# A two-layer decoder block on one core: the first layer's mixer, cross attention and routing issued in turns on half blocks, the shared expert divided over two places

## The chip, the cores and the metric

The kernel runs on one core of one Trainium2 chip. The metric is device time in microseconds (us) for one execution, the median of several runs. A profile is one execution recorded by the hardware profiler; its engines are PE (matmuls, with weight loads counted apart as PEld), DVE (vector), ACT (scalar and activation), POOL (general purpose) and SP (issues most transfers). "PE clock" is the share of full clock that the chip granted to PE.

## The reference

Input x is 64 sequences of 64 tokens with 256 features, all float32, and a context of 64 x 64 x 64. Two layers follow one another, each with three residual steps on a layer norm of x:

```python
x = x + ssm(layernorm(x))            # layer 0 mixer: in_proj, conv over 4 tokens, silu, chunked scan, out_proj
x = x + cross_attn(layernorm(x), ctx)# layer 0: 16 heads against the rotated context
x = x + moe(layernorm(x))            # layer 0: top 2 of 7 experts, and one shared expert for all tokens
x = x + rwkv(layernorm(x))           # layer 1: time mixing, a max-stabilised scan
x = x + gqa(layernorm(x), ctx, ctx)  # layer 1: 32 query heads, 8 key/value heads
x = x + ffn(layernorm(x))            # layer 1: 64 experts in 8 groups, dense over the groups
```

Each expert of `moe` is `down(silu(gate(u)) * u)` with `u = up(h)`, with a bias in each of the three. An expert's result is scaled by its token's probability; the shared expert's result is not.

## The kernel before

x (4096 tokens) stays in on-chip memory as 32 tiles of 128 tokens. A block is 512 tokens (`TB`, 8 blocks, `NBLK`), a half block 256 (`HT` in the new code). Matmul results go to PSUM tiles that rotate through one tag (`mm`); cross attention also had a tag of double size (`big`).

Three phases make the first layer, one after the other (`run`, `phase`, `moe_phase`). In them the program states work in a pipeline's order, and the framework's scheduler decides in what order instructions stand on each engine.

- **Mixer** (to 395 us). `ssm_front` works on a block: layer norm and RMS norm (`norm`, on POOL, L107), transposes (`transposed`, L116), projections of 512 columns (`proj`, L210), convolution (`acc`, ACT L236, DVE L239), softplus (L169 to L180), Silu (L240, L242). Then per tile `ssm_mix`, `ssm_scan` and `ssm_out`. The weights of cross attention are combined beside it (`prep_xattn`).
- **Cross attention** (395 to 810 us). `xattn_front` per block: the rotated context `kv` and its transpose, the norm (`ln_T`), queries (`q_ps`, L374). Per tile `xattn_scores`, `xattn_turn`, `xattn_values`, `xattn_out` (L414). Meanwhile `moe_clear` writes zeros over the whole row buffer `moe_hs` in DRAM, 30 pieces of 1088 KB.
- **Experts** (810 to 1229 us). `moe_front` routes a block: norm, transposes, router logits (`pl`, L496), choice of two experts on DVE (L503 to L509), ranks within each expert by two matmuls (`rk`, L519, L520), probabilities, slots. Eight scatters on POOL (L541) then put each row into its expert's part of `moe_hs`. When all blocks are routed, `moe_tables` computes which expert each tile of 256 slots belongs to. `moe_fetch` reads two numbers of that table on SP, then loads the rows (`ht`) and the expert's weights (`pack`). There are 38 routed tiles (`MAXT`) with stages `moe_turn`, `moe_up` (L618), `moe_gate` (L627), `moe_down` (L638, L646), which write `moe_ys` in DRAM. The shared expert is 16 further tiles in the same stages: 14 ahead of the routed ones, beside the routing, and 2 after. All biases of the last product come by one more matmul with the probabilities (`prT`, `moe_bd`, L640).

The second layer (`layer1`) follows from 1229 us on. It is issued by hand: inside `manual_schedule()` every engine executes in program order. Each part is a generator that yields between pieces, and `beside` takes pieces from several generators in proportion to the counts given. First `collect_block(0)` gathers expert results into x (L693, POOL), then `wkv(0)` runs alone, then `wkv(1)` beside `gqa(0)`; these make the ramp, to 1441 us. After that `ffn_block(b)`, `wkv(b + 2)` and `gqa(b + 1)` run beside one another. `ffn_front` at the end of `gqa` makes the norm `fr_h` on POOL (L1022), its transposes (L1028), and the gating, with waiting turns (`rest`) between its pieces.

Of the kernel before, what the change touches and what calls it, by code (L numbers as in the profile page):

```python
# [6 lines left out]
F32 = mybir.dt.float32  # L7
# [6 lines left out]
P = 128  # L14
# [5 lines left out]
HB = NB // 2  # L20
NBLK = 8
LN_EPS = 1e-5
# [4 lines left out]
SLOTS = NBLK * TB  # L27
ET_PER_E = SLOTS // ET
MAXT = (2 * SLOTS + 7 * (ET - 1)) // ET
# [13 lines left out]
class Net:  # L43
# [32 lines left out]
    def big(self, shape, name):  # L76

        return self.pp.tile(shape, F32, tag="big", bufs=self.n_big, name=name)

    def open_psum(self, n_big):  # L80
        self.n_big, self.n_mm = n_big, 8 - 2 * n_big
        self.pp = self.tc.alloc_tile_pool(name="psum", bufs=1, space=PSUM, reuse_waits="tile")
# [21 lines left out]
    def norm(self, wk, blk, rs, nm, eng):  # L104
        h = wk.tile([P, NT, D], F32, tag="h", bufs=2, name="h")
        for t in range(NT):
            eng.tensor_scalar(h[:, t], self.x[:, blk * NT + t], rs[:, t:t + 1], nm[:, t:t + 1], ALU.mult, ALU.add)  # L107
        return h

    def transposed(self, h):  # L110

        out = []
        for c in range(2):
            ps = self.mm([P, TB], "hT_ps")
            for t in range(NT):
                self.nc.tensor.transpose(ps[:, t * P:(t + 1) * P], h[:, t, c * P:(c + 1) * P], self.ident)  # L116
            out.append(ps)
        return out

    def ln_T(self, wk, blk, eng):  # L120
        nc = self.nc
        mv, rs = self.stats(wk, blk * NT)
        nm = self.neg_mean_times(wk, mv, rs)
        h = self.norm(wk, blk, rs, nm, eng)
        ps = self.transposed(h)
        hT = wk.tile([P, 2, TB], F32, tag="hT", bufs=2, name="hT")
        nc.scalar.copy(hT[:, 0], ps[0])  # L127
        nc.vector.tensor_copy(hT[:, 1], ps[1])
        return hT
# [30 lines left out]
    def softplus(self, wk, dt, raw):  # L160

        nc = self.nc
        sh = [P, NT, 4]

        def t(n):
            return wk.tile(sh, F32, tag="sp_" + n, bufs=2, name="sp_" + n)
# [15 lines left out]
    def ssm_front(self, wk, w, blk):  # L182
        nc, te = self.nc, self.nc.tensor
        mv, rs = self.stats(wk, blk * NT)
        nm = self.neg_mean_times(wk, mv, rs)

        r2 = wk.tile([P, NT], F32, tag="r2", bufs=2, name="r2")
        nc.vector.tensor_mul(r2, rs, rs)
        nc.vector.tensor_mul(r2, r2, mv[:, :, 1])
        nc.vector.tensor_scalar(r2, r2, RMS_EPS, None, ALU.add)  # L190
        rr = wk.tile([P, NT], F32, tag="rr", bufs=2, name="rr")
        nc.gpsimd.tensor_tensor(rr, r2, self.mhalf, ALU.pow)
        nc.vector.tensor_mul(rr, rr, rs)
        nr = self.neg_mean_times(wk, mv, rr, "ln_nr")
        h = self.norm(wk, blk, rr, nr, nc.gpsimd)
        r1 = wk.tile([P, NT], F32, tag="r1", bufs=2, name="r1")
        nc.vector.tensor_scalar(r1, rs, 1.0, None, ALU.add)
        ps = self.transposed(h)
        hT = wk.tile([P, 2, TB], F32, tag="hT", bufs=2, name="hT")
        nc.scalar.copy(hT[:, 0], ps[0])  # L200
        nc.vector.tensor_copy(hT[:, 1], ps[1])

        for t in range(NT):
            n = blk * NT + t
            nc.gpsimd.tensor_scalar(self.x[:, n], self.x[:, n], r1[:, t:t + 1], nm[:, t:t + 1], ALU.mult, ALU.add)

        def proj(col):
            ps = self.mm([P, TB], "proj")
            for c in range(2):
                te.matmul(ps, w["in"][:, c, col:col + P], hT[:, c], start=c == 0, stop=c == 1)  # L210
            return ps


        pdt = self.mm([P, NT, 4], "pdt")
        for t in range(NT):
            for c in range(2):
                te.matmul(pdt[:, t], hT[:, c, t * P:(t + 1) * P], w["in"][:, c, 1024:1028], start=c == 0, stop=c == 1)
        raw = wk.tile([P, NT, 4], F32, tag="raw", bufs=2, name="raw")
        nc.vector.tensor_add(raw, pdt, bc(w["dtb"], 1, NT))
        dt = wk.tile([P, NT, 4], F32, tag="dt", bufs=2, name="dt")  # L220
        self.softplus(wk, dt, raw)
        la = wk.tile([P, NT, 4], F32, tag="la", bufs=2, name="la")
        nc.vector.tensor_mul(la, dt, bc(w["A"], 1, NT))

        bT = wk.tile([P, TB], F32, tag="bT", bufs=2, name="bT")
        cT = wk.tile([P, TB], F32, tag="cT", bufs=2, name="cT")
        nc.scalar.copy(bT, proj(1028))
        nc.vector.tensor_copy(cT, proj(1156))

        sg = wk.tile([P, 4, TB], F32, tag="sg", bufs=2, name="sg")  # L230
        xs = wk.tile([P, 4, TB], F32, tag="xs", bufs=2, name="xs")
        g2 = wk.tile([P, 4, TB], F32, tag="g2", bufs=2, name="g2")
        for q in range(4):
            px = proj(512 + q * P).rearrange("p (b s) -> p b s", s=S)
# [104 lines left out]
    def xattn_kv(self, wk, w, blk):  # L339
# [5 lines left out]
        for j in range(2):  # L345
            self.load(c2[j * S:(j + 1) * S], cv)
# [1027 lines left out]
```

## Time and profile before

| what | us |
|---|---|
| median of 3 runs (2395.75 to 2404.59) | 2399.03 |
| the profiled execution, its whole time | 2401.51 |
| its span, first to last instruction | 2399.7 |
| PE busy over the span | 2084.6 (87%) |
| DVE, ACT, POOL busy | 1257.5, 775.1, 804.0 |
| mean PE clock granted | 0.929 |

An engine's busy time is the union of its instructions' intervals. A group's mean is the duration of one instruction; matmuls overlap in the pipeline, so a 256-column matmul lasts 379 ns while the next starts 215 ns after it. A float32 matmul stands as two records. "Idle before" is how long the engine had nothing before an instruction, with what released it.

### The profile page before, as it was taken

The numbers are of one execution on the slowest core, as the hardware profiler recorded it, in microseconds if no ns is written. First come the engines' busy times: TensorE is split into PE (matmuls) and PEld (weight loads), VectorE is DVE, ScalarE is ACT, GpSimd is POOL, SyncE is SP. The second block draws the span as 40 slices with busy tenths as digits, with TensorE's granted clock in tenths as the row PEclk, the third lists the DMA queues.
The fourth block names the chain that finished last, engine by engine and source line by source line (L and its number), as shares of the span: only waits on it lengthen the run. The fifth ranks groups of instructions, "written<-read, shape, count | busy, mean of one in ns | idle before, by whom it ended". The sixth has DMA issues, their size and how long they took to land.

```text
span 2399.7 us, 32463 instructions
## 1 busy us (share of the span) xinstructions
PE 2084.6 (87%) x12586; PEld 1487.4 (62%) x12586; DVE 1257.5 (52%) x2832; ACT 775.1 (32%) x1398; POOL 804.0 (34%) x1047
## 2 busy tenths in 40 slices
PE   6899998999999667999954659888898989898989
PEld 3566665566666556888853446556666656565666
DVE  5565566544444433333326556555666656665332
ACT  2232241222223243333312214334342434353421
POOL 4434435322222353011144634252525243332100
PEclk8899999999999768999986779999999999999999
DMA  4111006660000111367751101010101010000000
GB/s 136 32 31 31 1 1 200 190 214 5 1 1 1 37 70 50 119 223 242 232 147 28 25 3 19 8 25 5 30 6 29 3 23 12 12 6 12 6 5 11
DMA packets 111514, 133.81 MB, mean 56 GB/s; under 512 B 31866, under 2 KB 100610, under 8 KB 111362
## 3 DMA queue, kind: packets, MB, share of 16 engines
q1 hardware_dynamic: 96034, 104.48, 14.2%
q0 software_dynamic: 15328, 27.27, 4.5%
q8 instruction: 99, 1.62, 0.3%
q14 instruction: 53, 0.43, 0.1%
HBM read 75.23 MB, written 56.49 MB: 55 GB/s over the span
## 4 chain that ended last, share of the span: by engine, by line
PE 53%; DVE 16%; POOL 13%; issue 13%; ACT 3%; DMA 1%; POOLq 0%; DVEq 0%; SPq 0%; ACTq 0%
PE gu_ps L1096 10%; PE proj L210 5%; PE q_ps L374 4%; PE acc L1130 4%; POOL x_sb L693 3%; PE po L414 3%; PE po L280 2%; PE sc L384 2%; POOL moe_hs L541 2%; PE pc L408 2%; PE st L935 2%; PE gu_ps L1102 2%; DVE ln_st L91 1%; PE wk_po L839 1%; POOL ln_rs L96 1%
## 5 line engine op out<-in xcount | busy, mean ns | idle before, releaser
L1096 PE MATMUL gu_ps<-ffn_gu,hT 128*128 128x352 f32 x1024 | 333.7, 472 | 7.3 <-DVE gqa_q L924 6.9
L1096 PEld LDWEIGHTS gu_ps<-ffn_gu,hT 128*128 128x128 f32 x1024 | 192.1, 195 | 109.3 <-issue 12.0
L1107 DVE SCALAR_TENSOR_TENSOR a<-a,fr_sca,gu_ps 128x176 f32<-128x176 f32 x256 | 84.6, 392 | 165.1 <-ACT a L1106 164.8
L1130 PE MATMUL acc<-ffn_d,aT 128*128 128x256 f32 x704 | 166.0, 385 | 0.0
L210 PE MATMUL proj<-hT,w_in 128*128 128x512 f32 x320 | 146.8, 616 | 0.0
L1130 PEld LDWEIGHTS acc<-ffn_d,aT 128*128 128x128 f32 x704 | 130.6, 192 | 20.2 <-issue 4.5
L1106 ACT ACTIVATE a<-gu_ps 128x176 f32<-128x176 f32 x256 | 60.5, 322 | 235.7 <-PE gu_ps L1102 235.7
L629 DVE TENSOR_TENSOR gT<-gT,uT 128x512 f32<-128x512 f32 x54 | 37.4, 692 | 166.7 <-ACT gT L628 166.7
L393 POOL TENSOR_TENSOR p<-p,sm 128x1024 f32<-128x1024 f32 x32 | 60.9, 1902 | 186.1 <-DVE sm L392 186.1
L414 PE MATMUL po<-xa_vo,ctxT 128*128 128x256 f32 x512 | 117.6, 379 | 0.0
L374 PE MATMUL q_ps<-hT,xa_q 128*128 128x512 f32 x256 | 113.8, 602 | 1.5 <-ACT hT L127 1.4
L414 PEld LDWEIGHTS po<-xa_vo,ctxT 128*128 128x128 f32 x512 | 96.3, 190 | 25.8 <-issue 12.2
L693 POOL DMA_INDIRECT x_sb<-moe_ys,left x64 | 102.6, 1604 | 21.3 <-issue 18.7
L647 POOL DMA_DIRECT2D moe_ys<-y x38 | 27.2, 717 | 238.3 <-DVE y L646 231.3
L210 PEld LDWEIGHTS proj<-hT,w_in 128*128 128x128 f32 x320 | 61.8, 197 | 72.3 <-issue 69.2
L924 DVE TENSOR_REDUCE gqa_q<-sc 128x8 f32<-128x512 f32 x128 | 79.3, 681 | 23.3 <-PE sc L922 22.8
L961 POOL TENSOR_TENSOR x_sb<-x_sb,at 128x256 f32<-128x256 f32 x32 | 24.8, 776 | 197.7 <-DVE at L960 197.7
L541 POOL DMA_INDIRECT moe_hs<-moe_h,moe_slots x64 | 62.3, 974 | 74.8 <-issue 35.5
L255 POOL TENSOR_TENSOR ul<-ssm_U,la 128x512 f32<-128x512 f32 x32 | 34.0, 1064 | 158.0 <-PE pld L257 158.0
L374 PEld LDWEIGHTS q_ps<-hT,xa_q 128*128 128x128 f32 x256 | 48.4, 192 | 61.6 <-issue 55.6
L96 POOL TENSOR_TENSOR ln_rs<-ln_ve,mhalf 128x4 f32<-128x4 f32 x40 | 40.9, 1022 | 118.8 <-DVE ln_ve L94 100.9
L938 ACT ACTIVATE pT<-st 128x512 f32<-128x512 f32 x128 | 66.1, 602 | 38.0 <-PE st L935 37.8
(334 smaller groups left out, 4677.5 us busy)
## 6 DMA issues: line engine op xcount, KB each, us to landing
moe_hs<-moe_zero SPq DMA_DIRECT2D x30, 1088.0 KB, 11.2
pack<-in_moe_pack_dram SPq DMA_DIRECT2D x38, 770.0 KB, 5.5
ht<-moe_hs SPq DMA_DIRECT2D x38, 272.0 KB, 2.9
moe_ys<-y POOLq DMA_DIRECT2D x38, 256.0 KB, 5.6
c<-in_ctx_dram SPq DMA_DIRECT2D x40, 128.0 KB, 3.5
x_sb<-in_x_dram SPq DMA_DIRECT2D x8, 512.0 KB, 8.7
out_dram<-x_sb SPq DMA_DIRECT2D x32, 128.0 KB, 1.7
ffn_gu<-in_ffn_guT_dram SPq DMA_DIRECT2D x8, 352.0 KB, 7.9
```

What stands on the lines that cost most here:

```text
L96: nc.gpsimd.tensor_tensor(rs, ve, self.mhalf[:, 0:nt], ALU.pow)
L210: te.matmul(ps, w["in"][:, c, col:col + P], hT[:, c], start=c == 0, stop=c == 1)
L374: te.matmul(ps, wq[:, c, hp * P:(hp + 1) * P], hT[:, c], start=c == 0, stop=c == 1)
L393: nc.gpsimd.tensor_mul(p, p, bc(sm, 2, S))
L414: self.nc.tensor.matmul(po, st["cT"][:, hp], w["vo"][:, hp], start=hp == 0, stop=hp == 7)
L541: s = gp.indirect_dma_start(w["hs"], bass.IndirectOffsetOnAxis(w["slots"][:, b, k, i:i + 1], 0), ha[k][:, i], None).ins
L693: self.nc.gpsimd.indirect_dma_start(self.x[:, b * NT + i], None, self.ys, bass.IndirectOffsetOnAxis(self.left[:, b, k, i:i + 1], 0), compu ...
L924: v.tensor_reduce(st["qa"][:, :, k, 16:18], sc[k], AX.X, ALU.max, negate=True)
L938: self.nc.scalar.activation(pT[:, k], ps[k].rearrange("p j g s -> p j (g s)"), AF.Exp, scale=8.0 ** -0.5)
L1096: te.matmul(ps, f["hT"][:, c, tok], w["gu"][:, 4 * q + j, c], start=c == 0, stop=False)
L1107: v.scalar_tensor_tensor(a[:, e], a[:, e], f["sca"][:, k:k + 1], pg[j][:, 176:352], ALU.mult, ALU.mult)
L1130: self.nc.tensor.matmul(self.acc, aT, w["d"][:, k], start=k == 0, stop=k == 10)
```

## The change

The three phases of the first layer become one function `layer0` inside `manual_schedule()`, so every engine follows program order there. It takes 18 steps (`NH + XLAG`, `NH` = 16 half blocks). In step n it issues, in proportion: the mixer of half block n with the front of half n + 1, cross attention of half n - 2 with the front of half n - 1, and half of the routing of a block whose halves are done. In the first two steps the combination of cross attention weights runs in place of cross attention. All tiles are sized to a half block: projections and queries are 256 columns wide, two to a PSUM tile; cross attention's PSUM tiles of double size are divided. Norms of mixer and cross attention move to ACT (`normed`); `kv` is kept in two standing tiles that are cleared once.

The routing of blocks 0 to 6 thus lies in `layer0`; block 7's comes at the start of `moe_phase`. Each routed block's transposed rows are stored to DRAM (`hTd`) and loaded again by the shared expert. `moe_clear` goes: two pieces are cleared at the start, and `moe_tables` scatters 14 rows-of-zero tiles behind the last row of each expert. The bias matmuls and `prT` go: a routed tile loads its expert's bias (with the shared one added), DVE adds it and ACT scales. The shared expert has 6 tiles (`EARLY`) ahead of the routed ones, and 10 in `moe_rest`, issued beside the ramp of the second layer. The last layer's weights are loaded inside that ramp (`load_ffn`). In `moe_phase` SP alone follows program order. In `ffn_front` one waiting turn between `fr_h` and its transposes becomes four.

```diff
+EARLY = 6
+NH = 2 * NBLK
+XLAG = 2
-    def ssm_front(self, wk, w, blk):
+    def ssm_front(self, wk, w, n0, f):
...
+        def proj(*cols):
+            ps = self.mm([P, 2, HT], "proj")
+            for i, col in enumerate(cols):
+                for c in range(2):
+                    te.matmul(ps[:, i], w["in"][:, c, col:col + P], hT[:, c], start=c == 0, stop=c == 1)
             return ps
...
+            for i in range(2):
+                nc.scalar.activation(a[:, i], px[:, i], AF.Identity, bias=w["cb"][:, q + i:q + i + 1], scale=w["cw"][:, 3, q + i:q + i + 1])
+                for k in (2, 1, 0):
+                    m = 3 - k
+                    v.scalar_tensor_tensor(a[:, i, :, m:], px[:, i, :, :S - m], w["cw"][:, k, q + i:q + i + 1], a[:, i, :, m:], ALU.mult, ALU.add)
+            yield
...
+    def ssm_half(self, wk, w, n):
+        f, nf = self.sf, {}
+        front = self.ssm_front(wk, w, 2 * n + 2, nf) if n + 1 < NH else iter(())
...
+        yield from self.in_turns(tiles(), front)
...
+    def xattn_half(self, wk, w, n):
+        f, nf = self.xf, {}
+        front = self.xattn_front(wk, w, n + 1, nf) if n + 1 < NH else iter(())
...
+            for t in range(2):
+                for g in range(2):
+                    self.xattn_scores(wk, w, f, t, st[t], g)
+                    yield
+                self.xattn_softmax(wk, st[t])
+            yield
...
-    def moe_clear(self, w, k):
-        if k < ROWS // (8 * P):
-            self.load(w["hs"][k * 8 * P:(k + 1) * 8 * P].rearrange("(p i) d -> p i d", i=8), bc(w["zero"], 1, 8))
...
         for k in range(2):
             for i in range(NT):
-                s = gp.indirect_dma_start(w["hs"], bass.IndirectOffsetOnAxis(w["slots"][:, b, k, i:i + 1], 0), ha[k][:, i], None).ins
+                yield
+                gp.memset(w["gap"], 0.0)
+                self.moe_row(w, w["slots"][:, b, k, i:i + 1], ha[k][:, i])
...
+        tl, ti = t("tl", [P, 7, 2]), wk.tile([P, 7, 2], I32, tag="mt_ti", bufs=1, name="mt_ti")
+        v.tensor_add(tl, bc(cnt, 2, 2), bc(w["slot"], 2, 2))
+        v.tensor_add(ti, tl, bc(w["pos"], 1, 7))
+        for e in range(7):
+            for i in range(2):
+                self.moe_row(w, ti[:, e, i:i + 1], w["zero"])
...
+        b = st["b"] = wk.tile([P, D], F32, tag="bias", bufs=6, name="bias")
+        nc.sync.dma_start(b, w["bias"][bass.ds(e, 1)].rearrange("o n -> (o n)").partition_broadcast(P))
...
+        nc.vector.tensor_add(y, ps, bc(st["b"], 1, 2))
         for i in range(2):
-            nc.vector.tensor_scalar(y[:, i], ps[:, i], st["h"][:, i, D:D + 1], None, ALU.mult)
+            nc.scalar.activation(y[:, i], y[:, i], AF.Copy, scale=st["h"][:, i, D:D + 1])
...
-        order = [("s", n) for n in range(14)] + [("r", j) for j in range(MAXT)] + [("s", n) for n in range(14, 16)]
+        for _ in self.moe_front(wk, w, NBLK - 1):
+            pass
+        self.moe_tables(wk, w)
+        order = [("s", n) for n in range(EARLY)] + [("r", j) for j in range(MAXT)]
...
+        with self.tc.manual_schedule(engines={self.nc.sync.engine}):
+            for k in range(len(order) + len(stages) - 1):
+                if k >= EARLY - 2 and fetched < MAXT:
+                    for _ in range(3 if k == EARLY - 2 else 1):
+                        self.moe_fetch(wk, w, fetched, tiles[fetched])
+                        fetched += 1
...
-        yield
+        yield from self.rest(4)
         hT = f["hT"] = wk.tile([P, 2, TB], F32, tag="hT", bufs=2, name="hT")
...
         with self.tc.manual_schedule():
-            for _ in self.collect_block(0):
-                pass
-            beside((wkv(0), 1))
-            beside((wkv(1), 43), (gqa(0), 73))
+            more = self.moe_rest(wk)
+            next(more)
+            beside((self.collect_block(0), 8), (itertools.islice(more, 10), 10))
+            beside((wkv(0), 51), (itertools.islice(more, 20), 20), (self.load_ffn(w_ffn), 10))
+            beside((wkv(1), 43), (gqa(0), 79), (more, 60))
...
+    def layer0(self, wk, w_ssm, w_xattn, w_moe):
+        self.sf, self.xf = {}, {}
+        route = iter(())
+        with self.tc.manual_schedule():
+            for _ in self.ssm_front(wk, w_ssm, 0, self.sf):
+                pass
+            for n in range(NH + XLAG):
+                streams = []
+                if n < NH:
+                    streams.append((self.ssm_half(wk, w_ssm, n), 18))
+                if n < 2:
+                    ready = self.in_turns(*(self.prep_xattn(wk, w_xattn, 2 * n + k) for k in range(2)))
+                    if n == 1:
+                        ready = itertools.chain(ready, self.xattn_front(wk, w_xattn, 0, self.xf))
+                    streams.append((ready, 28))
+                m = n - XLAG
+                if m >= 0:
+                    streams.append((self.xattn_half(wk, w_xattn, m), 23))
+                if m >= 2:
+                    if m % 2 == 0:
+                        route = self.moe_front(wk, w_moe, m // 2 - 1)
+                    streams.append((itertools.islice(route, 15) if m % 2 == 0 else route, 15))
+                self.beside(*streams)
```

## The prediction

> **What bounds the kernel now.** I read the windows first, cut where the stages change (the first matmul of each stage in the timeline), then the waits of the matmul engine PE in the poor windows, then the groups that the change touches. Columns: window, its length, then busy us (and instructions) of PE, weight loads, DVE, ACT, POOL, the granted PE clock, DMA share, GB/s.
>
> ```profile
> 0.00:46.00 46.00, 27.91 (x71) 14.54 (x71) 24.60 (x85) 10.87 (x17) 18.23 (x29) 0.99 0.60 177
> 46.00:395.00 349.00, 330.87 (x1450) 222.70 (x1451) 206.94 (x522) 102.42 (x155) 152.75 (x168) 0.91 0.09 27
> 395.00:810.00 415.00, 386.35 (x2288) 261.09 (x2287) 208.70 (x313) 113.74 (x143) 116.44 (x91) 1.00 0.27 81
> 810.00:965.00 155.00, 99.80 (x444) 86.54 (x445) 65.27 (x366) 60.35 (x103) 70.79 (x74) 0.69 0.17 60
> 965.00:1229.00 264.00, 264.00 (x1301) 227.86 (x1300) 97.85 (x186) 87.86 (x185) 26.53 (x37) 1.00 0.57 192
> 1229.00:1441.00 212.00, 108.94 (x711) 77.52 (x710) 115.16 (x204) 43.90 (x79) 109.52 (x147) 0.70 0.21 47
> 1441.00:2280.00 839.00, 756.34 (x5799) 521.06 (x5801) 506.03 (x1062) 330.76 (x651) 305.82 (x497) 0.97 0.07 14
> ```
>
> Mixer (to 395) and cross attention (to 810) already keep PE 93 to 95% busy: little to win inside them. The experts (965 to 1229) are PE alone, 100%. The two holes are the routing (810 to 965: 99.8 of 155 us at clock 0.69) and the second layer's ramp (1229 to 1441: 108.9 of 212 us at 0.70). Who holds PE there, and in the woven part (line waiting <- releaser: us, times, longest):
>
> ```profile
> PE rk L519 <- DVE mr_sel L523: 16.6, 3, 6.0
> PE rk L519 <- DVE mr_both L513: 14.9, 4, 5.8
> ...
> PE wk_hT L739 <- ACT wk_h L734: 43.0, 7, 31.8
> PE pk L759 <- DVE wk_mix L752: 17.0, 4, 5.9
> PE wk_po L839 <- POOL wk_o L833: 15.5, 4, 8.0
> ...
> PE hT_ps L1028 <- POOL fr_h L1022: 27.0, 10, 6.3
> ```
>
> Both holes are chains of small DVE, POOL and ACT steps with too little PE work beside them. The rows that price the moved parts:
>
> ```profile
> L541 POOL DMA_INDIRECT moe_hs<-moe_h,moe_slots x64 | 62.3, 974 | 74.8 <-issue 35.5 <-DVE mr_sel L549 19.0 <-DVE moe_h L537 18.4
> L240 ACT ACT_TABLE_LOAD x8 | 10.3, 1283 | 14.8 <-DVE acc L239 14.8
> L239 DVE SCALAR_TENSOR_TENSOR acc<-proj,ssm_vec,acc 128x504 f32<-128x504 f32 x32 | 23.5, 736 | 8.0 <-ACT acc L236 8.0
> ```
>
> [...] clock 0.50 at 820 to 860 us, where PE was busy 7.7 and 9.1 of 20 us, and 1.00 through the experts. So a filled hole also makes the matmuls in it faster. [...] The trace shows weight loads starting about 0.2 us ahead of their matmul (L638, 941.37 against 941.58). [...] The trace shows the 1283 ns [...] (the load at 46.67 is followed by work at 47.96), so I charge 1.28 us.
>
> **The change part by part.** The sum is made against the profiled execution: 2401.5 us, span 2399.7, of which 1.8 us lies outside; it stands 2.5 us (0.1%) above the median of 2399.0.
>
> Narrower matmuls. Two records of 512 columns become four of 256. Four 256-column records take 0.86 us in the experts' timeline (0.215 each), one of 512 takes 0.43 in the mixer's (24.70, 25.13, 25.56): PE loses nothing, though the list of instructions grows from 7187 to 7411 matmuls.
>
> First layer, PE work. 27.9 + 330.9 + 386.4 = 745 us; seven of eight routings come in. One is 2.2 us for 16 pl records, 1.04 for 8 transposes and 0.6 for rk: 3.9, so 27 for seven. The mixer's clock of 0.91 should rise to about the 0.97 of the woven layer, some 12 us back. About 760.
>
> First layer, fill. The nearest row for three streams in hand-written order is the second layer's: 756.3 of 839, 0.90. I take it. Other engines leave room: DVE in 0 to 810 is 440 us, plus seven eighths of the routing's 65 less its shared tiles (about 50), plus fixed costs of halving. These are 96 convolution operations of 0.73 that become 192 of about 0.42 (+11), 18 softplus and 8 norm operations more per half at 0.17 (8 halves, +35), and a share of the copies (+22): 560 of some 870, 64%, like the second layer's 60%. ACT takes about two table loads a half, 32 against 16: +20. POOL has 287 us in 0 to 810 and gains 24 power operations of 1.0 and seven blocks of scatters (56 x 1.26 = 71, with 0.1 memsets in their gaps): some 390 of 870, hidden. The start stays alone: half a front runs before anything beside it, about 28 us with 8 of PE. In the last two steps only cross attention is left (386/16 = 24 us of PE each): I estimate 30 each. Between: (760 - 8 - 48)/0.90 = 782. End of the first layer at 28 + 782 + 60 = **870 us**, where before it was 810 with the routing still to come.
>
> Handover to the experts. The last block's routing cannot be woven. From the last addition to x: statistics, power, norm, transposes, pl and the choice took 16 us by the steps in the timeline (811 to 816, 944 to 954). Then 8 scatters, and 14 new scatters of zero rows that replace 28 of the 30 cleared 1088 KB pieces, all on POOL at 0.96 plus 0.30 us of gap: 22 x 1.26 = 28. Landing 2.5, then on SP the fetch (2.9 for rows, 5.5 for the pack, a new 128 KB bias load between them, I count 7 together). First routed tile 54 us after the first layer. Six shared tiles of 5.2 us (the 6.05 us cadence less 4 records of bias) should cover it, but the fetches of three tiles stand ahead of the loads of shared tiles 4 and 5 in SP's order, so only four cover: 21 us. The rest is idle, at low clock. Then 2 x 5.2 + 38 x 5.63 + 4 = 228. The bias addition is one DVE operation of 0.69 and two ACT operations of 0.47 for two DVE of 0.48; DVE is 37% busy there, no cost. Experts end at 870 + 54 + 228 = **1152**, against 1229: -77.
>
> Ramp. Ten shared tiles bring 52 us of PE into 103 idle, 14 us of DVE (one product and one addition of 0.69 a tile), 40 ACT operations of 0.47 (19), and table loads as Silu meets Exp, up to 20 x 1.28 = 26. The chain there is DVE and POOL, DVE 54% busy; so I charge **+15**. Ends: -10, if the warmer clock shortens the 109 us of PE, and +45, if all ACT work lands on the chain. Sixteen loads of 256 KB and the ffn weights move into SP's order; the DMA share there is 0.21, so nothing.
>
> Second layer. Four idle turns now stand between fr_h and its transposes. That may free up to the 27.0 us in the row above, but the later front may come late for the next block (weT_ps and smT_ps waited 11.7 and 9.9 already). Ends -25 and +10; I take **-5**.
>
> Sum: -77 + 15 - 5 = -67. 2401.5 - 67 = 2334.5, and against the median **2332**.
>
> **Rivals.**
> (a) The first layer fills worse, and it ends slower. Place: DVE's queue in each half step. There 12 convolution operations (5 us) and then a softplus chain of 18 (3.2 us, with a trip to ACT for Exp behind Silu, 1.28 or more) stand ahead of copies that PE waits for (qT, pT, ctxT). For it: strict order, and the DVE load above the second layer's. Against: these copies are used one to three turns later, 2 us each. A step costs 782/14 = 56 us here; the 67 us are gone at 5 us more a step, a fill of 0.83. At 63 us a step: 2332 + 98 = 2430.
> (b) It fills as the old mixer did, 0.95: 741 instead of 782, so 2291. For it: 8 PSUM buffers and three independent streams. Against: the second layer never got there.
> (c) The layer fills at 0.90, but the handover runs cold (+15) and the ramp pays all its ACT work (+45 instead of +15): 2377. For it: ACT holds wk_hT 43 us today.
> (d) The split does not cover what it says: if the four early tiles wait for the last hT store on SP, 21 us more are bare: 2353.
>
> **How the numbers follow.** My case with (d) has 0.47, (b) 0.17, (c) 0.14, (a) 0.22. A measurement of this kernel can tell about 0.5%, 12 us. Faster by more: mine, (b) and 0.11 of (c), 0.75. Within: 0.07, from the edges of (c) and (a). Slower: the other 0.18 of (a). The range goes from (b) with most of the second layer's gain, 2275, to (a) at about 63 us a step, 2428; some 0.08 lies below and 0.10 above.
>
> **What would show it.** Right: PE fill near 0.90 and clock above 0.95 to about 870 us, no window at clock 0.5 except some 30 us ahead of the experts, experts still 5.6 us a tile, ramp PE clock above 0.8. Wrong: first layer past 950 us with PE waiting on DVE copies (a); or a ramp over 240 us (c).

## The result, and the profile after

The changed kernel takes **2542.39 us** (median of 4 runs, 2537.82 to 2547.72) where the kernel before takes 2397.78 (median of 4 runs): ratio 1.0599, interval 1.0567 to 1.063. It is 6% slower; the forecast was 2332. The profiled execution is 2544.7 us, with a span of 2543.0.

The marks below are the first or last matmul of a stage, the same in every kernel: the last `po` of cross attention, the first `ht_ps`, the last routed `d_ps`, the first `gu_ps`.

| stage | forecast | after | difference |
|---|---|---|---|
| start and 16 steps with a mixer | 28 + 782 = 810 | 925.5 | +115.5 |
| last two steps | 60 | 82.0 | +22 |
| handover, to the first routed tile | 54 | 72.1 | +18 |
| experts | 228 | 234.6 | +7 |
| ramp (212 before) | 227 | 241.0 | +14 |
| second layer (959 before) | 954 | 987.8 | +34 |

The differences make 210 us, and 2544.7 less the forecast's 2334.5 is 210 too. Every stage missed in the same direction, two thirds of it in the first layer.

The windows of the changed kernel, divided at these marks (columns as before: window, length, busy us and instructions of PE, weight loads, DVE, ACT, POOL, then granted clock, DMA share, GB/s):

```profile
28.00:925.50 897.50, 739.85 (x4159) 598.82 (x4160) 553.57 (x1500) 272.35 (x445) 313.88 (x374) 0.87 0.09 25
925.50:1007.50 82.00, 65.20 (x369) 50.21 (x367) 41.18 (x98) 17.49 (x29) 23.86 (x40) 0.83 0.08 29
1007.50:1079.60 72.10, 37.41 (x127) 29.45 (x127) 16.11 (x67) 13.63 (x26) 25.51 (x31) 0.69 0.52 179
1079.60:1314.20 234.60, 232.73 (x1113) 193.59 (x1111) 79.10 (x120) 104.06 (x232) 26.53 (x37) 1.00 0.70 209
1314.20:1555.20 241.00, 163.08 (x921) 116.94 (x922) 124.96 (x220) 75.73 (x129) 109.47 (x147) 0.82 0.23 53
1555.20:2543.00 987.80, 877.74 (x6329) 605.58 (x6327) 534.14 (x1160) 363.61 (x721) 318.58 (x503) 0.95 0.07 13
```

The first line is the woven first layer. PE is busy 739.85 of 897.50 us, a fill (busy share of PE) of 0.82 where 0.90 was assumed, and at a clock of 0.87 where I had hoped for 0.97. No other engine is full: DVE is at 62%. So this is not an engine at its limit on average. The waits of PE in the stretch 95 to 920 us say what it is (line that waits, releaser, us in all, times, longest):

```profile
PE sf_hT_ps L116 <- ACT sf_h L108: 99.0, 13, 9.0
PE xn_hT_ps L116 <- ACT xn_h L108: 34.8, 26, 6.4
PE pld L253 <- POOL ul L244: 7.1, 1, 7.1
```

Two releasers hold nearly all of it: the norms of the mixer's next half (`sf_h`) and of cross attention's next half (`xn_h`), just ahead of their transposes. In the old kernel `phase` issued the front of the next block three tiles ahead of its first use. In the new one a step begins with these norms. Two consecutive steps (364.5 to 424.5 and 424.5 to 480.9), divided into quarters:

```profile
364.50:379.50 15.00, 8.40 (x77) 5.49 (x76) 10.44 (x34) 4.02 (x6) 6.05 (x9) 0.82 0.00 0
379.50:394.50 15.00, 11.05 (x50) 9.28 (x51) 10.29 (x19) 6.97 (x13) 7.12 (x6) 0.72 0.01 2
394.50:409.50 15.00, 15.00 (x91) 12.94 (x90) 12.02 (x45) 5.71 (x11) 1.27 (x1) 1.00 0.14 44
409.50:424.50 15.00, 15.00 (x71) 12.47 (x69) 6.76 (x17) 3.51 (x6) 3.54 (x3) 1.00 0.01 1
424.50:438.60 14.10, 8.85 (x82) 6.01 (x80) 9.77 (x29) 3.53 (x5) 5.02 (x8) 0.88 0.04 10
438.60:452.70 14.10, 9.85 (x43) 8.29 (x44) 10.22 (x26) 4.92 (x9) 10.92 (x14) 0.76 0.08 29
452.70:466.80 14.10, 14.10 (x76) 11.58 (x76) 10.12 (x32) 6.19 (x11) 6.44 (x11) 1.00 0.11 41
466.80:480.90 14.10, 14.10 (x69) 11.85 (x69) 5.12 (x10) 2.28 (x5) 2.92 (x3) 1.00 0.03 11
```

This is the main reading of the case. The second half of each step is full (PE 100%, clock 1.00). The first half has PE 56 to 74% busy at a clock of 0.72 to 0.88, while DVE is 70% busy. A layer-wide 0.82 is the mean of two very different halves. The timeline of one such head shows the queue (start, length, engine, line, result, and in brackets the idle time before and its releaser):

```profile
433.11 0.70 POOL L183 TENSOR_TENSOR sf_rr<-sf_r,mhalf 128x2 f32<-128x2 f32 x1 [0.74 <-DVE sf_r L184]
...
437.23 1.22 DVE L445 TENSOR_REDUCE sm<-p 128x16 f32<-128x1024 f32 x1 [1.22 <-ACT p L443]
...
439.31 0.69 DVE L438 TENSOR_TENSOR p<-sc,mx 128x512 f32<-128x512 f32 x1
...
440.13 0.74 DVE L621 TENSOR_TENSOR mr_sel<-moe_oh,mr_slot 128x56 f32<-128x56 f32 x1
...
441.79 0.15 DVE L186 TENSOR_TENSOR sf_rr<-sf_rr,sn_rs 128x2 f32<-128x2 f32 x1
441.98 0.16 DVE L101 SCALAR_TENSOR_TENSOR sn_nr<-sn_mv,sf_rr 128x2 f32<-128x2 f32 x1
...
442.18 1.09 ACT L108 ACTIVATE sf_h<-x_sb,sn_nr,sf_rr 128x256 f32<-128x256 f32 x2 [4.98 <-DVE sn_nr L101]
442.83 1.40 PE L116 MATMUL sf_hT_ps<-ident,sf_h 128*128 128x128 f32 x4 [7.54 <-ACT sf_h L108]
```

The tiny `sn_nr` (0.16 us) that the norm needs is behind the softmax sum of cross attention, its scores and the routing in DVE's queue; ACT idles 4.98 us for it and PE 7.54. What it is made from, `sf_rr`, left POOL at 433.81 and was taken up 7.98 us later, though DVE stood idle for 1.22 us of them, waiting for `p`: here DVE kept to the order in which its work was issued.

The handover has two long waits of PE (from its waits in 920 to 1080 us):

```profile
PE u_ps L712 <- ACT uT L713: 13.2, 1, 13.2
PE u_ps L712 <- DMA sh_hT<-moe_hT: 10.6, 2, 9.6
```

The second is that for the loads of shared tiles 4 and 5; what the first waited for the trace does not show (see the last section). It is not what makes this handover long: e1 to e6 below, which issue this stage alike, don't have the first wait, but one of 25.7 to 26.9 us for the same loads in its place, and handovers of 69.7 to 71.4 us. In e1 (both waits for these loads together, the longest 26.2):

```profile
PE u_ps L719 <- DMA sh_hT<-moe_hT: 27.9, 2, 26.2
```

In the experts a routed tile takes 5.85 us instead of the 5.62 of a tile without bias matmuls before. The two scalings that moved to ACT stand ahead of `uT` there, and PE's weight loads wait for `uT` (1080 to 1310 us, then one tile on ACT); in the kernel before they wait for nothing in this stage (990 to 1200 us):

```profile
PEld u_ps L712 <- ACT uT L713: 13.3, 35, 0.6
...
1202.75 0.91 ACT L737 ACTIVATE y<-y,ht 128x256 f32<-128x256 f32 x2 [2.03 <-DVE y L735]
1203.57 0.45 ACT L713 ACTIVATE uT<-u_ps,pack 128x256 f32<-128x256 f32 x1
```

Of the 13.3 us of these waits some 8 lengthen the stage (37 intervals of routed tiles, 8.1 us above 5.62 each).

The second layer (PE's waits in 1555 to 2543 us):

```profile
PE hT_ps L1150 <- POOL fr_h L1144: 25.2, 17, 3.4
PE pq L1014 <- POOL gqa_q L1026: 20.5, 7, 3.7
PE smT_ps L1201 <- DVE ffn_soft L1196: 19.1, 7, 7.4
PE pk L876 <- DVE wk_mix L869: 14.1, 9, 2.9
```

The four rests ahead of `hT_ps` moved its wait from 27.0 to 25.2 us, next to nothing, and `pq`, `smT_ps` and `pk` grew from 9.5, 9.9 and 9.4. Of the groups of before, the scatters cost 986 ns each (974 before), but their idle time of 74.8 us is now 13.9 (last line); the convolution has its wait on ACT:

```profile
L217 DVE SCALAR_TENSOR_TENSOR sf_acc<-proj,ssm_vec,sf_acc 128x252 f32<-128x252 f32 (+2 forms) x192 | 91.2, 475 | 79.5 <-ACT sf_acc L214 74.9
L637 POOL DMA_INDIRECT moe_hs<-moe_h,moe_slots x64 | 63.1, 986 | 13.9 <-issue 12.9 <-DVE moe_h L628 0.7 <-ACT uT L713 0.3
```

### The profile page after: what moved, and what is told of

Read it like the earlier page. It is cut to its first block, busy times and chain, and to the rows that moved or that the text cites. A ratio compares the mean times of both kernels' runs of the same rounds, so it can differ in the third digit from the quotient of the medians.

```text
span 2543.0 us, 34282 instructions
## 1 busy us (share of the span) xinstructions
PE 2129.4 (84%) x13066; PEld 1605.5 (63%) x13066; DVE 1360.3 (53%) x3196; ACT 853.0 (34%) x1592; POOL 822.5 (32%) x1149
## 4 chain that ended last, share of the span: by engine, by line
PE 39%; DVE 10%; POOL 4%; ACT 2%; issue 2%; DMA 1%; SPq 0%; POOLq 0%; DVEq 0%; ACTq 0%
PE gu_ps L1218 11%; PE acc L1252 4%; PE u_ps L712 3%; PE d_ps L730 3%; PE g_ps L721 3%; PE gu_ps L1224 2%; PE wk_po L956 2%; DVE wk_er L945 2%; PE sc L1039 1%; DVE a L1229 1%; POOL x_sb L815 1%; PE pk L876 1%; PE st L1052 1%; PE pq L1014 1%; PE pv L876 1%
## 5 line engine op out<-in xcount | busy, mean ns | idle before, releaser
L1252 PE MATMUL acc<-ffn_d,aT 128*128 128x256 f32 x704 | 171.3, 394 | 0.0
L202 PE MATMUL proj<-sf_hT,w_in 128*128 128x256 f32 x640 | 160.8, 397 | 0.8 <-DVE sf_hT L195 0.8
L422 PE MATMUL q_ps<-xn_hT,xa_q 128*128 128x256 f32 x512 | 138.0, 419 | 3.9 <-DVE xn_hT L407 3.9
L202 PEld LDWEIGHTS proj<-sf_hT,w_in 128*128 128x128 f32 x640 | 125.7, 200 | 24.2 <-issue 3.1
L217 DVE SCALAR_TENSOR_TENSOR sf_acc<-proj,ssm_vec,sf_acc 128x252 f32<-128x252 f32 (+2 forms) x192 | 91.2, 475 | 79.5 <-ACT sf_acc L214 74.9
L723 DVE TENSOR_TENSOR gT<-gT,uT 128x512 f32<-128x512 f32 x44 | 30.5, 692 | 173.8 <-ACT gT L722 157.1
L422 PEld LDWEIGHTS q_ps<-xn_hT,xa_q 128*128 128x128 f32 x512 | 107.2, 216 | 25.5 <-issue 4.5
L116 PE MATMUL sf_hT_ps<-ident,sf_h 128*128 128x128 f32 x64 | 21.7, 447 | 114.4 <-ACT sf_h L108 114.1
L275 POOL TENSOR_TENSOR y<-y,sf_g 128x512 f32<-128x512 f32 x32 | 40.9, 1278 | 216.5 <-DVE y L274 216.2
L116 PEld LDWEIGHTS sf_hT_ps<-ident,sf_h 128*128 128x128 f32 x64 | 10.9, 205 | 123.3 <-ACT sf_h L108 123.2
```

The lines of the kernel that those rows point to most:

```text
L202: te.matmul(ps[:, i], w["in"][:, c, col:col + P], hT[:, c], start=c == 0, stop=c == 1)
L217: v.scalar_tensor_tensor(a[:, i, :, m:], px[:, i, :, :S - m], w["cw"][:, k, q + i:q + i + 1], a[:, i, :, m:], ALU.mult, ALU.add)
L422: te.matmul(ps[:, i], wq[:, c, hp * P:(hp + 1) * P], hT[:, c], start=c == 0, stop=c == 1)
L1252: self.nc.tensor.matmul(self.acc, aT, w["d"][:, k], start=k == 0, stop=k == 10)
```

## The experiments

Two theories stood at the start. **Theory**: the norm that is made at the head of a step stands late in DVE's queue and holds PE; each stage outside the first layer has a loss of its own. From e6 on it says more: the streams of a step all begin with their DVE-bound part. **Rival**: the first layer is bound by DVE's load, as rival (a) of the forecast had it, and a wait that is taken away only comes back at the next operand.

In the profiled runs, the first `po` of the mixer came at 81.9 us in the changed kernel, at 81.8 in e2, at 78.3 in e9 and 77.6 in e12, and at 74 to 76 in the others, though they begin nearly alike. The clock makes this difference: from 54 to 66 us PE is busy all the time in the changed kernel and in e4, at half clock in the first and at full clock in the second, where it gets through twice as many matmuls (43 and 92):

```profile
54.00:66.00 12.00, 12.00 (x43) 10.25 (x43) 3.60 (x8) 1.73 (x3) 1.26 (x1) 0.50 0.00 0
54.00:66.00 12.00, 12.00 (x92) 10.48 (x92) 7.52 (x17) 2.75 (x5) 1.27 (x1) 1.00 0.08 21
```

So I compare the lengths of stages and put the medians beside them. "First layer" here runs from the first `po` of the mixer to the last of cross attention, 81.9 to 1007.5 us in the changed kernel. The versions ran on five chips, on which the kernel before took 2399.6 to 2406.5; medians of different groups (e1 to e4, e5 to e8, e9 to e11, e12, e13 and e14) compare only to some 7 us.

| run | median us | first layer | handover | experts | ramp | second layer |
|---|---|---|---|---|---|---|
| changed kernel | 2542.39 | 925.6 | 72.1 | 234.6 | 241.0 | 987.8 |
| e1 | 2492.38 | 880.0 | 71.1 | 234.0 | 238.1 | 989.6 |
| e2 | 2518.02 | 908.4 | 70.4 | 234.0 | 236.4 | 989.9 |
| e3 | 2535.50 | 924.2 | 69.9 | 234.6 | 239.5 | 989.8 |
| e4 | 2513.96 | 925.8 | 69.7 | 234.6 | 235.8 | 969.5 |
| e5 | 2464.85 | 858.4 | 69.9 | 234.0 | 236.9 | 988.7 |
| e6 | 2498.30 | 889.6 | 71.4 | 234.0 | 237.7 | 987.8 |
| e7 | 2517.02 | 926.0 | 50.0 | 235.4 | 238.2 | 989.6 |
| e8 | 2529.02 | 926.6 | 91.8 | 234.1 | 211.6 | 989.1 |
| e9 | 2430.17 | 854.9 | 68.3 | 234.5 | 227.0 | 963.7 |
| e10 | 2421.22 | 850.9 | 65.0 | 234.0 | 227.1 | 967.2 |
| e11 | 2395.74 | 829.1 | 67.0 | 234.0 | 227.4 | 963.5 |
| e12 | 2417.92 | 852.6 | 50.7 | 236.1 | 231.8 | 967.3 |
| e13 | 2394.68 | 829.7 | 59.7 | 234.0 | 232.0 | 963.2 |
| e14 | 2399.31 | 836.1 | 52.9 | 234.0 | 232.0 | 966.8 |

**e1: the mixer's norm a step earlier.**

```diff
+        if n:
+            nf, front = self.early
+            front = itertools.chain(self.rest(2), front)
+        later = self.ssm_front(wk, w, 2 * n + 4, lf)
...
                 self.ssm_out(wk, w, 2 * n + t, st[t])
+                next(later, None)
```

> Edit: the statistics and the norm of the mixer's next half (the first two pieces of ssm_front) are issued one step earlier, beside the last two ssm_out; two empty turns stand in their old place, so every other instruction keeps its turn. Theory (the norm chain at the head of a step holds TensorE: 99.0 us of waits at sf_hT_ps, and the lower clock after them): first layer ends about 100 us sooner, near 905, time about 2440, sf_hT_ps waits under 15 us. Rival (the step is bound by the load of the VectorE queue, the wait only moves to the next late operand): first layer ends within 25 us of 1007, time above 2515, the waits reappear at proj, qT or pT.

The first layer fell by 46 us, half of what the theory said. Both theory and rival were partly right. The wait at `sf_hT_ps` is gone, but PE's waits in 95 to 900 us now read:

```profile
PE q_ps L429 <- DVE xn_hT L414: 51.1, 13, 5.7
PE xn_hT_ps L116 <- ACT xn_h L108: 38.9, 30, 6.4
```

The next operand in the same head took over: the copy `xn_hT`, in the same DVE queue behind the same softmax and routing.

**e2: three more turns ahead of cross attention's transposes**, on top of e1.

```diff
-        yield
+        yield from self.rest(4)
         ps = self.turned(h, "xn_hT_ps")
```

> Edit: as e1_norm_early, and three empty turns between the norm xn_h of cross attention and its transposes. Theory: the 34.8 us of waits at xn_hT_ps go too, first layer ends 25 to 35 us before that of e1_norm_early, time about 2410. Rival: the query matmuls come late for the scores of the next step instead, no gain or a loss over e1_norm_early.

The theory's number failed: 28 us worse than e1. The wait at `xn_hT_ps` went from 38.9 to 3.8 us, and `proj` waited 76.6 for DVE's copy `sf_hT` instead. My reading, which no run tests by itself: with the transposes moved later, the head had still less for PE to do, and moving a wait out of a head does not help if its work goes with it.

**e3: less DVE work** behind the norms. This kernel leaves out the convolution's additions and seven steps of the softplus.

```diff
-                for k in (2, 1, 0):
-                    m = 3 - k
-                    v.scalar_tensor_tensor(a[:, i, :, m:], px[:, i, :, :S - m], w["cw"][:, k, q + i:q + i + 1], a[:, i, :, m:], ALU.mult, ALU.add)
...
-        for k in (15, 13, 11, 9, 7, 5, 3):
-            nc.vector.scalar_tensor_tensor(p, p, 1.0 / k, z, ALU.add, ALU.mult)
```

> Leaves out part of the computation: the 12 convolution additions per half on VectorE and the 7 middle steps of the softplus polynomial, some 7 us of VectorE work in each of 16 steps (5.7 + 1.2). Forecast's rival (a) (these stand in the VectorE queue ahead of the copies that TensorE waits for): at least 5 us a step, 80 us or more, time at or below 2460. Theory (the wait is at the norm chain at the head of the step, where none of this work stands in front): under 30 us, time above 2510.

The first layer changed by 1.4 us, though DVE was busy some 100 us less in it (494 instead of 595 us). So the load of DVE does not bound this layer, and the convolution and the softplus, the very place named by the forecast's rival (a), cost nothing here. PE's wait at `sf_hT_ps` stayed at 99.1 us; whether this work would cost something once that wait is gone, e3 cannot say.

**e4: `ffn_front` as before**, and with it the counts by which the streams are issued.

```diff
-        yield from self.rest(4)
+        yield
...
-            beside((wkv(1), 43), (gqa(0), 79), (more, 60))
+            beside((wkv(1), 43), (gqa(0), 73), (more, 60))
...
-                beside((self.ffn_block(wk, w_ffn, b, fs), 33), (wkv(b + 2), 43), (gqa(b + 1), 77))
+                beside((self.ffn_block(wk, w_ffn, b, fs), 33), (wkv(b + 2), 43), (gqa(b + 1), 74))
```

> Edit: the second layer's ffn_front gets its one turn back between fr_h and the transposes (instead of four), and the weights of the streams are 73 and 74 again (instead of 79 and 77), all else as in the changed kernel. Theory (the rests push the later pieces of ffn_front and the key-value stream late: pq, smT_ps, pk waits grew by 11, 9 and 5 us): the second layer from 988 back to about 960, time about 2515. Rival (the second layer is longer because the shared tiles leave it later or colder, or because of placement in memory): no change within 8 us.

The second layer fell by 18 us and the ramp by 5; `smT_ps`, `pq` and `pk` are back at 9.6, 9.5 and 9.4. Some 10 us to the 959 of before remain; e9 and e13, with 963.7 and 963.2, leave 4. These are no longer waits: PE is idle 92 us in e4 as in the kernel before (110 in the changed one), but busy 877 us instead of 867 with the same matmuls, at a clock of 0.96 instead of 0.97. What makes the clock differ stays open.

**e5: one copy from DVE to ACT**, on top of e1.

```diff
         hT = wk.tile([P, 2, HT], F32, tag="xn_hT", bufs=1, name="xn_hT")
-        v.tensor_copy(hT, ps)
+        nc.scalar.copy(hT, ps)
```

> Edit: as e1_norm_early, and the copy of xn_hT from PSUM is done by ScalarE instead of VectorE, at the same place. In e1 TensorE waits 51.1 us for that copy, which stands in VectorE's queue behind the softmax sum and the routing. Theory (one operand in a strict VectorE queue): most of the 51.1 us go, time about 2450. Rival (the head of each step holds too little TensorE work that is ready, whatever the operand): the wait moves to the next operand, gain under 15 us.

The first layer fell by another 22 us, between the two expectations. PE's waits in 95 to 900 us:

```profile
PE xn_hT_ps L116 <- ACT xn_h L108: 38.7, 29, 6.4
PE proj L202 <- DVE sf_hT L195: 25.5, 5, 5.4
PE q_ps L429 <- ACT xn_hT L414: 19.3, 7, 3.0
```

The 51.1 us became 19.3 at the same place and 25.5 at `proj`, so most of the wait came back; yet one operand's place in DVE's queue is worth 22 us. The waits are shorter and more spread, and the clock in this stretch is 0.94, after 0.92 in e1 and 0.88 in the changed kernel (windows from 95 us to the last steps).

**e6: cross attention and routing half a step later**, on the changed kernel alone.

```diff
+            pad = itertools.chain.from_iterable
+            xs = pad(itertools.chain(self.xattn_half(wk, w_xattn, m), self.rest(1)) for m in range(NH))
+            xs = itertools.chain(self.rest(12), xs)
...
-                    streams.append((self.xattn_half(wk, w_xattn, m), 23))
+                    streams.append((itertools.islice(xs, 23) if n < NH + XLAG else xs, 23))
```

> Edit, on the changed kernel alone: cross attention and routing run half a step (12 of 23 turns) later than the mixer, all else as it was; the first layer gets half a step more at its end, some 15 us. Theory (the streams all start a step with their VectorE-bound part, so the first half of each 56 us step leaves TensorE 37% idle and the second half is full; apart they fill each other's gaps): steps of about 51 us, first layer ends near 955, time about 2490. Rival (the long chains wait wherever they stand): steps stay at 55 us or more, time 2540 or above.

The first layer fell by 36 us with no norm moved in its own stream, though it has half a step more at its end. The waits at `sf_hT_ps` fell from 99.0 to 3.9 us; `ssm_out` now waits 54 us for `y` and the scatters on POOL. So the same instructions cost less when the heads stand apart. The gain is smaller than the theory said, though: from the first `po` of one half to that of the next, the later steps (the fifth to the fourteenth such interval) take 56.1 us on average after 58.7, where the theory had some 51 and the rival 55 or more. In e13, with the norms early too, they take 51.4.

**e7 and e8: the shared tiles.** e7 issues the loads of the early tiles first; e8 also sets `EARLY = 16`.

```diff
+        early = [dense(n) for n in range(EARLY)]
         with self.tc.manual_schedule(engines={self.nc.sync.engine}):
...
-                        states[k] = dense(n) if kind == "s" else tiles[n]
+                        states[k] = early[n] if kind == "s" else tiles[n]
```

> Edit: the loads of all six early shared tiles are issued on SP ahead of the fetches of routed tiles (six buffers instead of two). Forecast's step (only four tiles cover, the last two wait behind three fetches on SP): first routed tile at about 57 us after the end of the first layer instead of 71.5, time about 2528. Rival (the routed tile waits for the scatters and its own fetch anyway): no change within 5 us.

> Edit: as e7, and all 16 shared tiles run ahead of the routed tiles, none in the second layer's ramp. Theory (in the ramp ten shared tiles cost 26 us instead of nothing, while here each costs its 5.2 us of TensorE, some of it in idle time): ramp near 212 again, experts' end 35 to 52 us later than in e7, time 2535 to 2555. Rival (the ramp is longer for another reason, such as the ffn loads or the turns of the streams): ramp stays near 235, time 2565 or above.

e7 shortened the handover by 22 us, more than the 14 expected. In the changed kernel, SP held the loads of tiles 4 and 5 behind three and four fetches (issued at 1062.87 and 1067.08, the first fetch at 1055.20), and PE's order has those tiles' matmuls ahead of the routed tile's. With e7 PE waits only 9.9 us, for the routed rows, where e1 to e6 wait some 26 for these loads. In e8 the ramp is 211.6 us, the 212 of before, and the handover 42 us longer than in e7:

```profile
1002.50:1094.30 91.80, 82.80 (x367) 70.63 (x368) 30.52 (x87) 32.52 (x66) 26.25 (x31) 0.91 0.51 173
...
1328.40:1540.00 211.60, 105.69 (x681) 74.19 (x682) 112.83 (x200) 43.76 (x79) 108.25 (x147) 0.67 0.15 27
```

The ten tiles cost the ramp 26.6 us (e7's 238.2 less 211.6). Early, they cost 41.8. So the ramp is the cheaper place for them, by 15 us, but no cheap one. A hole with PE at 106 of 212 us was no free room for 52 us.

**e9 to e11: the mends together.** e9 joins e5, e4 and e7 with `EARLY = 8`. e10 joins the shift of e6, e1, the same early norm for cross attention, e4 and e7, `EARLY = 8`, without the copy on ACT of e5. e11 adds one turn to e10 (and counts 19 turns for the mixer instead of 18):

```diff
                 self.ssm_scan(wk, w, f, t, st[t])
                 yield
+            yield from self.rest(1)
```

> Edit: e5 (norm of the mixer early, xn_hT on ScalarE), e4 (ffn_front and weights 73 and 74) and e7 (loads ahead on SP) together, and eight early shared tiles instead of six. Theory (the losses lie in separate stages and add up): the gains of the single runs, 77 + 28 + 25 us, and some 5 for two tiles moved from the ramp (2.7 each there) into the 9.9 us in which TensorE waits for the first routed tile in e7: about 2407. Rival (they overlap, a gain of one stage is given back in the next): 2430 or more.

> Edit: the half step shift of e6, with statistics and norm of the mixer and of cross attention each issued at the end of their half before, with e4, e7 and eight early shared tiles. Theory (phase of the streams and position of the norm chains are two parts of one cause, VectorE's queue at the head of a step): the first layer ends 15 to 30 us before that of e9, time 2380 to 2395, faster than the kernel before. Rival (what is left in the first layer is VectorE and GpSimd work in strict order wherever it stands, as y on GpSimd ahead of ssm_out in e6): 2405 or more.

> Edit: as e10, and one empty turn in the mixer between ssm_scan and ssm_out, where TensorE waited 54 us in e6 for y (GpSimd, behind its scatters). Theory: up to 40 us of these go, 5 to 25 us below e10. Rival (the next chain takes over): no gain over e10.

e9 came out at the rival's 2430. By stages, the mends kept their value in the first layer (854.9) and the second (963.7). So the number was the rival's, but not for its reason. What was missing is in the handover, 68.3 instead of some 60, with a stop of PE of 9.7 us (see the last section), and in my sum: it added differences of medians, and each of them holds the late start of the changed kernel once (81.9 us after 74.3 to 75.3 in e4, e5 and e7: 21 us in all, where e9 itself starts only 3.6 us sooner). In e10 the first layer is only 4 us shorter than in e9; its waits are at `ssm_out`, as its rival said. One empty turn ahead of `ssm_out` took 22 us more from it (e11).

**e12 to e14: what is left.** e12 has two turns there and six early tiles; e13 one turn and six tiles; e14 is e13 with this line:

```diff
-        nc.gpsimd.tensor_add(y, y, f["g2"][:, :, tok])
+        nc.vector.tensor_add(y, y, f["g2"][:, :, tok])
```

> Edit: as e11, with two empty turns between ssm_scan and ssm_out instead of one, and six early shared tiles instead of eight (e9 to e11 show a handover of 65 to 68 us with eight, e7 one of 50 with six). Theory: handover about 50 instead of 67, ramp 8 us longer, the waits at ssm_out (52 us in e11) at 30 or below, first layer 10 to 20 us shorter: time about 2375. Rival (the waits at ssm_out are GpSimd's own backlog of scatters, which another turn does not shorten): first layer as in e11, time about 2387.

> Edit: as e11, with six early shared tiles instead of eight, so that e12 differs from it by the second empty turn alone. Theory (the two stages are separate: e12 lost 23 us in the first layer by its second turn and gained 16 us in the handover by the six tiles): first layer 829 as in e11, handover about 50 as in e12, ramp 4 us longer, time about 2384. Rival (the first layer of e12 was longer because of where the six-tile version places things, not by the turn): first layer about 850, time about 2417.

> Edit: as e13, and the second half of y (adding g2 to the product) is done by VectorE instead of GpSimd. Theory (GpSimd's scatters of 1.26 us each stand ahead of y, so TensorE waits at ssm_out, 52 us in e11): most of that goes, first layer 20 to 40 us shorter, time 2345 to 2365. Rival (VectorE's queue is the tighter one in this layer, as the forecast's rival (a) had it in kind: 32 more operations of some 0.7 us there cost what they give): first layer within 10 us of e13 or longer.

e12 contradicted its theory: the second empty turn made the first layer 23 us longer. e13 confirms that it was the turn (with its count), since with one turn the layer is 829.7 again. The second turn left PE's waits at `ssm_out` as they were (48.5 us, after 51.5 with one turn), and those at `pld` for scatters on POOL grew from 2.6 to 12.0 us, which is less than half of the 23. e14 went to its rival: PE's wait at `ssm_out` for `y` is still 50.7 us, now from DVE instead of POOL, so the wait is no backlog of scatters alone. e13's handover, 59.7, missed the 50 of e7 and e12, again with a stop of PE, of 13.1 us.

**The best version** is e13: 2394.68 us against 2406.52 for the kernel before on the same chip, ratio 0.9943, interval 0.993 to 0.9957. It is 0.6% faster than the kernel before, and 6% faster than the changed one. e11 (ratio 0.9952, interval 0.9933 to 0.997, on another chip) is not told apart from it. The woven part of the first layer in the changed kernel and in e13, and then some 52 us of e13, about one step, in quarters:

```profile
95.00:920.00 825.00, 683.83 (x3881) 553.20 (x3881) 519.88 (x1400) 256.15 (x419) 292.36 (x349) 0.88 0.05 15
95.00:820.00 725.00, 656.33 (x3870) 531.66 (x3868) 516.79 (x1388) 289.00 (x442) 290.80 (x343) 0.95 0.05 17
400.00:413.00 13.00, 13.00 (x122) 10.97 (x121) 10.78 (x35) 7.13 (x10) 1.31 (x3) 1.00 0.01 1
413.00:426.00 13.00, 9.44 (x40) 7.71 (x39) 11.53 (x36) 4.95 (x7) 6.04 (x7) 0.87 0.03 11
426.00:439.00 13.00, 12.55 (x60) 8.99 (x59) 8.79 (x14) 4.88 (x9) 10.14 (x16) 1.00 0.12 44
439.00:452.00 13.00, 13.00 (x78) 10.91 (x76) 7.20 (x19) 3.15 (x6) 9.12 (x13) 1.00 0.09 32
```

656.33 of 725 is a fill of 0.905 at a clock of 0.95, after 0.83 at 0.88. One poor quarter is left in a step where there were two, and DVE is busier than before (71% of these 725 us after 63%). The forecast's fill of 0.90 was reachable, though not in the order that the change wrote. Its time was not: e13 is 63 us above the 2332, and its first layer ends at 904.7 us instead of 870.

## Why the prediction was wrong

- **First layer, fill: the step that failed.** I took 0.90 from the second layer, "the nearest row for three streams in hand-written order". The fill is a property of the order, not of hand-written orders: 0.82 as written, 0.905 with the same streams in e13. Worked out, 704 us of PE at 0.824 is 854 us, 72 more than the 782. PE's busy time was 739.85 instead of 704, at a clock of 0.87; that is another 36 / 0.824 = 44. Together 116. "12 us back" from a warmer clock had the wrong sign: the heads ran at a clock of 0.72 to 0.88.
- **Its rival (a)** had the right kind of cause (one operand late in DVE's queue, DVE well below full) and, at 2430, the right side. Its fill of 0.83, at which by the forecast's own sum the whole gain is gone, is the one that came (0.82); the lower clock came on top. Its "strict order" was my estimate; in the head above it is measured, 7.98 us for `sf_rr`. It named the wrong place: convolution and softplus (e3: 1.4 us) instead of the norms and copies at a step's head (e1, e5, e6: 46, 22 and 36 us). I had followed the chain inside one stream and not asked what the other streams put in front of it at that moment. It had 0.22. Of the other rivals, (b) with a fill of 0.95 did not come; (c) had a handover 15 us and a ramp 30 us longer, where 18 and 14 came, but no loss in the first layer; (d) did not come, since PE ran the first four shared tiles during the scatters.
- **Last two steps**: 82 us instead of 60. I had taken 24 us of PE and 6 of wait a step, with "only cross attention" left. But the routing of block 6 stands in these two steps too. PE was busy 65.2 us, at a clock of 0.83.
- **Handover**: 72 instead of 54. That tiles 4 and 5 stand behind the fetches on SP was seen, and charged as idle time beside the routed tile's fetch. What I missed is that PE's own order puts these tiles ahead of the routed one, so their late loads delay it (e1 to e6: one wait of some 26 us; e7, with the loads ahead: 22 us shorter).
- **Experts**: 234.6 instead of 228. The bias addition was charged at "no cost" because DVE had room; the two scalings on ACT delay `uT`, and a tile takes 5.85 us instead of 5.62, some 8 us in all.
- **Ramp**: "+15" measured 26.6 (e8 against e7), inside the ends of -10 and +45. Table loads on ACT came as feared, though fewer: 11 in the ramp of the changed kernel and 1 in that of e8, so 12.8 us more. How they and the other parts add up to 26.6 was not tested part by part.
- **Second layer**: "-5" has the wrong sign: 29 us longer than before. Undoing the rests, with the counts of the streams, gave back 18 (e4), which is PE's added idle time. The forecast named `smT_ps` as what could come late, and then charged the gain; it did (9.9 to 19.1).
- **Narrower matmuls at nothing**: not tried alone. In the full quarters PE is 100% busy at a clock of 1.00, so nothing there speaks against it.

The range ended at 2428, 114 us short. Its upper end was rival (a) alone, a loss in the first layer with all other stages as forecast. But first layer, handover and second layer each lost by an operand that stands late in an order written by hand (e1 and e6, e7, e4), and the range had no case in which these losses come together.

## What to carry to other kernels

When streams are woven by hand, divide one step of the profile into quarters: a mean fill (0.82 here) hides a head that is bound by small operations of another engine (PE 56 to 74% busy) and a tail that is full (100%). Start what a step's first transposes need in the step before, and start the streams at different phases, so that one stream's chain lies beside another's matmuls. In the order written here a late operand held up ACT by 4.98 us and PE by 7.54 (`sn_nr`), and late fetches on SP held up the loads behind them (tiles 4 and 5; with the loads ahead, e7, the handover was 22 us shorter). Price each edit by what is in front of it in every queue at that moment, and expect part of a removed wait to come back at the next operand of the same stretch (of 99 and 51 us of waits, e1 and e5 gained 46 and 22).

## What was not expected of the hardware

- The granted clock in a head that is 56 to 74% busy is 0.72 to 0.88, and 1.00 in the quarter after it. So in these steps a partly filled stretch of 15 us costs twice, in idle time and in slower matmuls.
- A full stretch does not always bring the clock back so soon. At the start of the changed kernel PE was busy without a break from 48.3 us on and stood at a clock of 0.50 until 67, some 19 us; in e4, with nearly the same matmuls, the clock was 1.00 from 54 to 66. The 6 to 8 us between them are lost in a stretch that looks 100% busy. What decides it stays open.
- In the handovers of the changed kernel, of e9 to e11, e13 and e14, PE stood still 7.5 to 13.2 us between shared tiles, from e9 on with their loads issued long before (in e11 all eight by 913.5 us; in e13 the stop begins at 935.6); the profile gives "issue" or ACT as the releaser there, and for ACT something "remote". The other versions have no such gap. The cause stays open.
- One empty turn in the mixer changed the first layer by -22 us, and the next one by +23. Of the second, the waits at `pld` account for some 9; the rest was not settled.
